# A four-layer graph attention kernel: sources listed from tile 1 on, 17 gather buffers, layer 0's masks kept beside its features

## The chip, the cores and the metric

One core of a Trainium2 chip runs the kernel. The metric is the device time of one execution in microseconds, as a median over runs; lower is better. Five engines work side by side, each in the order of its own instructions: PE multiplies matrices, DVE does elementwise work and reductions, ACT does activations and copies, POOL here mostly issues gathers, and SP issues the other transfers. Engines wait for one another through semaphores.

## The reference

A graph of 4,096 nodes with 256 features goes through four attention layers over one adjacency matrix. Edges are drawn with a probability that falls with both node numbers, so the first nodes have many neighbours and the late ones few. Each layer normalises the nodes, clips at zero, and adds the attention output to the nodes:

```python
_w = (1.0 + jnp.arange(4096)) ** -0.5
_w = _w / _w.mean()
adj = uniform((4096, 4096)) < clip(0.00390625 * _w[:, None] * _w[None, :], 0, 1)
...
h = jnp.maximum(_layernorm(x, axis=-1), 0.0)
...
h = node_features @ W.T + b_W
e = (h @ a1)[:, None] + (h @ a2)[None, :] + b_a[0]
e = jnp.where(e > 0, e, 0.2 * e)
scores = jnp.where(adjacency_matrix > 0, e, NEG_INF)
h_prime = jax.nn.softmax(scores, axis=1) @ h
...
x = x + h_prime
```

Layer 0 is the form shown. Layer 1 has no bias and puts an elu behind. Layer 2 has four heads of 64 features. Layer 3 takes a softmax of the scores and one of the negated scores, both over the projected inputs, and an elu; in the kernel these are two heads of 256.

## The kernel before

**Tiles.** 4,096 nodes are 32 tiles of 128 (NT), in 8 blocks of 512 targets (IB, NIB) and 8 chunks of four source tiles (CH, NCH). A node's row holds its features and, per head, two exponentials that stand in for the source's part of the score; `grow` holds the target's part, spread over partitions by a transpose on PE (L966) and an exponential on ACT (L972). One *step* takes 128 sources: DVE makes weights from `grow`, the row's exponential and a 0/1 mask (L1032; in layer 2 also ACT at L1018 and DVE at L1041 for two of the four heads), and PE multiplies them with the rows into an accumulator (L1068, in layer 2 L1093). A float32 matmul appears in the trace as two records.

**Dense blocks and listed tiles.** The first DENSE = (4, 2, 1, 1) target blocks of layers 0 to 3 are dense: they run over all 32 source tiles, 512 targets at a time. Every later target tile T is *listed*: it runs DP steps over the first DP source tiles, whose rows and masks lie in SBUF (`L.g` in layer 0, `L.pre` later, masks in `mpre`), and then CAPS[T] steps over lists of its actual sources. DP is 4, one chunk. `listed_sources` (L1208) fetches each list step with an indirect DMA on POOL (L1228): 128 rows of the layer's table in DRAM, at addresses from `index[T]`. A list shorter than its 128 x CAPS[T] places is filled with a row of zeros. If a list does not fit, a flag makes a slower program compute everything again.

**The lists.** While layer 0 runs, the adjacency arrives as int32 chunks (L1303), is made into bytes (L1322), stored to DRAM (L1324), and reduced to "does source p have any target in this tile" (L1329). From that `list_sources` (L819) counts places with matmuls, makes one-hot tiles on DVE (L875) in two halves of the JT = NT - DP source tiles, and multiplies them on PE (L900) into the index lists. These are used by all four layers.

**Masks.** A list step needs the 128 x 128 mask of its sources. For target blocks 1 to 3 the bytes lie beside the features in the tables of layers 1 and 2 (MASKS_IN, L473), so that one gather in the first listed layer of such a tile brings row and mask, and ACT copies the mask into `mlist` for later layers (L1240). For blocks 4 to 7, which are first listed in layer 0, masks lie in tensors of their own, `mask_t`; `gather_masks` (L922) fetches each with a second, small gather (L928), one per dense step ahead and the rest when the tile comes.

**Order.** `run` (L1191) walks a hand-written plan of (unit, step) pairs: fetch comes first, `begin` two, `weigh` three and `multiply` six plan places later (LEAD). POOL's instructions stand exactly in that order. In layer 0 the plan has 128 dense steps; from dense step LISTED0 = 40 on, each is followed by one or two listed steps in turn, and what is left runs alone. `sides` (L1284) says at which dense steps the chunks of blocks 4 to 7 are loaded: 2, 5, 8, ... 95. In layers 1 to 3 the plan starts with some dense steps alone (16, 36, 16) and spreads the rest over the first 24, 14 and 28 listed tiles; `all_sources` (L1413) streams their rows and masks chunk by chunk through SP, except for the first DP tiles. Gathered rows of layer 0 use a pool of 7 buffers (L1252), of layers 1 to 3 a pool of 9 (L1395). A buffer is free once PE, and where a mask is copied ACT, has read it.

Of the kernel before, what the change touches and what calls it, by code (L numbers as in the profile page):

```python
# [8 lines left out]
F32 = mybir.dt.float32  # L9
F16 = mybir.dt.float16  # L10
U8 = mybir.dt.uint8
# [6 lines left out]
P = 128  # L18
# [6 lines left out]
CH = 4  # L25
# [430 lines left out]
DP = CH  # L456
JT = NT - DP
TS0 = IT
# [3 lines left out]
LISTED0 = 40  # L462
CAPS = (25, 17, 15, 13, 12, 11, 11, 10, 10, 9, 9, 9, 8, 8, 8, 8) + (8,) + (7,) * 7 + (6,) * 8
# [9 lines left out]
MASKS_IN = {1: (2, False), 2: (1, False), 3: (1, True)}  # L473
FRONT = tuple(MW * ((l, False) in MASKS_IN.values()) for l in range(4))
TW = tuple(FRONT[l] + GW[l] + MW * ((l, True) in MASKS_IN.values()) for l in range(4))
# [4 lines left out]
def list_layers(ctx: ExitStack, tc: tile.TileContext, a: dict, out: bass.AP, flag):  # L480
# [29 lines left out]
    for T in range(TS0, NT):  # L510
# [8 lines left out]
    table = [dram.tile([N + 1, TW[l]], F32, name=f"table{l}", tag=f"table{l}") for l in range(4)]  # L519
    mask_t = {  # L520
        b: dram.tile([N + 1, IB], U8, name=f"mask_t{b}", tag=f"mask_t{b}")
        for b in range(NIB)
        if b not in MASKS_IN
    }
# [7 lines left out]
    def feature_rows(l, jt):  # L532
        return table_rows(table[l], jt)[:, :, FRONT[l] : FRONT[l] + GW[l]]

    def mask_rows(b, jt):
        if b not in MASKS_IN:
            return table_rows(mask_t[b], jt)
        l, behind = MASKS_IN[b]
        c0 = FRONT[l] + GW[l] if behind else 0
        return table_rows(table[l], jt)[:, :, c0 : c0 + MW].bitcast(U8)  # L540
# [6 lines left out]
    def weights(l, pool, prep, q):  # L547
# [11 lines left out]
        L.table = table[l]  # L559
# [123 lines left out]
    def node_rows(L, T0):  # L683
# [29 lines left out]
        for k, T in enumerate(tiles):  # L713
# [3 lines left out]
            hT = rows.tile([P, 2, P], F32, name=f"s_hT_{u}_{k}", tag="hT")  # L717
# [69 lines left out]
    def list_constants(pool):  # L787

        place = pool.tile([P, P, JT // 2], F16, name="place")
        nc.gpsimd.iota(  # L790
            place, pattern=[[1, P], [0, JT // 2]], base=0, channel_multiplier=0, allow_small_or_imprecise_dtypes=True
# [11 lines left out]
        n = (NT // 2 - DP) * IT  # L803
        for part, tiles, base in ((code[:, 0:n], NT // 2 - DP, DP * P - HALF), (code[:, n:], NT // 2, 1)):
            nc.gpsimd.iota(
                part,
                pattern=[[CH * P, tiles // CH], [1, CH], [0, IT]],
                base=base,
                channel_multiplier=CH,
                allow_small_or_imprecise_dtypes=True,  # L810
            )
# [7 lines left out]
    def list_sources(ib, seen, pool, consts):  # L819
# [3 lines left out]
        half = JT // 2  # L823
# [48 lines left out]
        def one_hot(T, j):  # L872

            first = pool.tile([P, P, half], F16, name=f"first_{T}_{j}", tag="first", bufs=2)
            nc.vector.tensor_tensor(  # L875
                first,
                place,
                lof[:, T % IT, j : j + half].unsqueeze(1).to_broadcast([P, P, half]),
# [5 lines left out]
        ahead = [(ib * IT + t, j) for t in range(IT) for j in (0, half)]  # L884
        firsts = [one_hot(*ahead[0])]
        yield 4.0
        for t in range(IT):
# [3 lines left out]
            for j in range(JT):  # L891
                if j % half == 0:
# [5 lines left out]
                if ps is None:  # L898
# [3 lines left out]
                    lhsT=first[:, :, j % half],  # L902
# [12 lines left out]

    masks_of = [
        (T, k)
        for T in range(DENSE[0] * IT, NT)
        for k in range(CAPS[T])
    ]  # L920

    def gather_masks(n, tile=None):  # L922

        for T, k in list(masks_of):
            if not n or tile is None and T not in index:
                break
            if tile in (None, T):
                nc.gpsimd.indirect_dma_start(  # L928
                    out=mlist[:, OFFS[T] + k, :],
                    out_offset=None,  # L930
                    in_=mask_t[T // IT],
                    in_offset=bass.IndirectOffsetOnAxis(ap=index[T][:, k : k + 1], axis=0),
                    element_offset=T % IT * P,
                )
                masks_of.remove((T, k))
                n -= 1

# [42 lines left out]
    class Unit:  # L980
# [4 lines left out]
        def __init__(u, L, T0, nt, n, get, big=None, heads=None, like=None, cost=1.7, nact=0, rates=(2, 0, 0), per=1):  # L985
# [205 lines left out]
    def run(plan):  # L1191

        n = len(plan)
        for p in range(n + LEAD[3]):
# [5 lines left out]
            if p >= LEAD[3]:  # L1200
# [4 lines left out]
                gather_masks(u.rates[2])  # L1205


    def listed_sources(L, T, pool):  # L1208
        heads = list(range(L.H))

        def get(i):
# [3 lines left out]
            else:  # L1215
# [4 lines left out]
                at, behind = MASKS_IN.get(T // IT, (0, False))  # L1220
                own = at == L.l > 0
                if at == 0:
                    gather_masks(CAPS[T], T)
# [7 lines left out]
                    in_=L.table,  # L1231
                    in_offset=bass.IndirectOffsetOnAxis(ap=index[T][:, k : k + 1], axis=0),
                    element_offset=FRONT[L.l] - front,
# [11 lines left out]
    with ExitStack() as phase:  # L1245
# [17 lines left out]
        def zero_rows():  # L1263
# [3 lines left out]
            for b in mask_t:  # L1267
                nc.sync.dma_start(mask_t[b][HALF : HALF + 1, :], zero[:, 0 : IB // 4].bitcast(U8))
            for l in range(4):
# [14 lines left out]
        sides = [2 + 3 * k for k in range((NIB - DENSE[0]) * NCH)]  # L1284
# [26 lines left out]
        def mask_chunk(ib, c):  # L1311

            load()
            if ib == 0:
                behind(c)
            m = (
                mpre[:, :, ib * IB : (ib + 1) * IB]
                if c == 0
                else mpool.tile([P, CH, IB], U8, name=f"s_m_{ib}_{c}", tag="m")
            )  # L1320
            for h, raw in enumerate(loaded[ib, c]):
                nc.vector.tensor_scalar(m[:, h * half : (h + 1) * half, :], raw, 0.0, None, op0=ALU.is_gt)  # L1322
            if c > 0 or ib in MASKS_IN:
                nc.sync.dma_start(mask_rows(ib, c * CH), m)  # L1324
            if ib > 0:
                if c == 0:
                    seen[ib] = lists_p.tile([P, JT, IT], F32, name=f"seen_{ib}", tag="seen", bufs=4)
                else:
                    nc.vector.tensor_reduce(  # L1329
                        seen[ib][:, (c - 1) * CH : c * CH, :].rearrange("p j t -> p (j t)"),  # L1330
                        m.rearrange("p j i -> p (j i)")
                        .bitcast(I32)
# [210 lines left out]
```

## Time and profile before

| | |
|---|---|
| median of 3 runs | 1810.38 us (1797.26 to 1814.76) |
| profiled execution | 1796.08 us, its span 1794.3 us |
| mean granted PE clock | 0.97 |
| PE, PE weight load, DVE, ACT, POOL busy | 93, 77, 74, 35, 54% |
| gathers of rows (L1228) | 715, mean 1060 ns on POOL |
| gathers of masks (L928) | 105, mean 1162 ns on POOL |
| copies of masks (L1240) | 113, mean 294 ns on ACT |
| steps on the fixed four tiles, DVE (L1032, 128x128) | 544 from `pre`, 64 from layer 0's `g` |
| DMA | 274.70 MB, mean 153 GB/s |

"Busy" is the share of the span in which an engine has an instruction under way. PE's matmuls are pipelined, so the duration of one record is longer than the time between two. POOL's time for a gather is the time in which it issues the transfer; the data land later.

### The profile page before, as it was taken

The numbers are of one execution on the slowest core, as the hardware profiler recorded it, in microseconds if no ns is written. First come the engines' busy times: TensorE is split into PE (matmuls) and PEld (weight loads), VectorE is DVE, ScalarE is ACT, GpSimd is POOL, SyncE is SP. The second block draws the span as 40 slices with busy tenths as digits, with TensorE's granted clock in tenths as the row PEclk, the third lists the DMA queues.
The fourth block names the chain that finished last, engine by engine and source line by source line (L and its number), as shares of the span: only waits on it lengthen the run. The fifth ranks groups of instructions, "written<-read, shape, count | busy, mean of one in ns | idle before, by whom it ended". The sixth has DMA issues, their size and how long they took to land.

```text
span 1794.3 us, 29158 instructions
## 1 busy us (share of the span) xinstructions
PE 1660.2 (93%) x9268; PEld 1384.3 (77%) x9268; DVE 1319.1 (74%) x3908; ACT 631.0 (35%) x1915; POOL 960.5 (54%) x930
## 2 busy tenths in 40 slices
PE   6998899799889999888999999988889999999997
PEld 4886777678778778676577878788888888888876
DVE  6787899777744676556788888877785566777755
ACT  5630010020120232333467666788884011111101
POOL 8836666646535656553353444444561666655453
PEclk9999999999879999989999999999999999999999
DMA  7888778853244444543233332323342665666553
GB/s 258 301 299 281 242 244 251 264 143 110 60 135 138 134 117 134 147 132 106 82 94 86 90 90 81 98 82 83 99 116 75 197 208 175 183 180 178 160 165 107
DMA packets 152237, 274.70 MB, mean 153 GB/s; under 512 B 21423, under 2 KB 75340, under 8 KB 152076
## 3 DMA queue, kind: packets, MB, share of 16 engines
q0 software_dynamic: 45584, 130.39, 26.8%
q1 hardware_dynamic: 105656, 141.83, 24.2%
q8 instruction: 77, 1.26, 0.3%
q14 instruction: 84, 0.69, 0.1%
q10 hardware_dynamic: 836, 0.53, 0.1%
HBM read 231.76 MB, written 40.90 MB: 152 GB/s over the span
## 4 chain that ended last, share of the span: by engine, by line
PE 78%; DVE 8%; issue 4%; DMA 3%; POOL 3%; ACT 2%; another core or an unknown queue 2%; SPq 0%; POOLq 0%; DVEq 0%; ACTq 0%
PE s_acc L1068 44%; PE s_accm L1093 20%; PE s_pj L748 8%; DVE s_p L1032 3%; PE idx_ps L900 2%; PE s_tp L716 2%; PE s_sT L966 2%; DMA s_gg<-table,idx 1%; DMA s_raw<-in_adjT 1%; ACT s_p L1018 1%; DVE s_m L1322 1%; POOL s_z L702 1%; POOL s_gg L1228 1%; DVE s_p L1041 0%
## 5 line engine op out<-in xcount | busy, mean ns | idle before, releaser
L1228 POOL DMA_INDIRECT s_gg<-table,idx x715 | 757.9, 1060 | 733.5 <-PE s_acc L1068 228.6
L1032 DVE SCALAR_TENSOR_TENSOR s_p<-s_grow,s_gg,mlist 128x128 f32<-128x128 f32 x994 | 310.1, 346 | 143.0 <-PE s_acc L1068 85.9
L1068 PE MATMUL s_acc<-s_gg,s_p 128*128 128x257 f32 x1430 | 353.8, 390 | 9.9 <-DVE s_p L1032 7.8
L1068 PEld LDWEIGHTS s_acc<-s_gg,s_p 128*128 128x128 f32 x1430 | 270.5, 194 | 53.6 <-DVE s_p L1032 12.6
L1068 PE MATMUL s_acc<-g,s_p 128*128 128x257 f32 x1152 | 292.5, 397 | 14.2 <-DVE s_p L1032 5.3
L1068 PEld LDWEIGHTS s_acc<-g,s_p 128*128 128x128 f32 x1152 | 220.0, 198 | 49.7 <-issue 12.3
L1032 DVE SCALAR_TENSOR_TENSOR s_p<-s_grow,pre,mpre 128x128 f32<-128x128 f32 (+1 forms) x576 | 189.2, 369 | 49.4 <-PE s_acc L1068 30.5
L1093 PE MATMUL s_accm<-s_p,s_gg 128*65 128x128 f32 x1744 | 204.7, 273 | 1.7 <-issue 1.6
L1068 PE MATMUL s_acc<-s_gs,s_p 128*128 128x257 f32 x896 | 203.6, 380 | 0.0
L1032 DVE SCALAR_TENSOR_TENSOR s_p<-s_grow,s_gs,s_ms 128x512 f32<-128x512 f32 x224 | 161.9, 748 | 50.7 <-PE s_accm L1093 24.7
L748 PE MATMUL s_pj<-s_w,s_hT 128*128 128x259 f32 (+3 forms) x640 | 175.9, 417 | 24.9 <-ACT s_hT L718 9.5
L1093 PEld LDWEIGHTS s_accm<-s_p,s_gg 128*65 128x65 f32 x1744 | 193.2, 138 | 5.3 <-issue 2.8
L1018 ACT ACTIVATE s_p<-s_grow,s_minus,s_gg 128x128 f32<-128x128 f32 x436 | 186.7, 485 | 25.9 <-PE s_accm L1093 15.0
L1068 PE MATMUL s_acc<-pre,s_p 128*128 128x257 f32 x768 | 184.0, 384 | 5.5 <-ACT s_y L1179 3.5
L1068 PEld LDWEIGHTS s_acc<-s_gs,s_p 128*128 128x128 f32 x896 | 169.4, 190 | 24.7 <-issue 0.6
L972 ACT ACTIVATE s_grow<-s_sT 128x256 f32<-128x256 f32 (+2 forms) x136 | 46.8, 367 | 379.3 <-PE s_sT L966 260.9
L748 PEld LDWEIGHTS s_pj<-s_w,s_hT 128*128 128x128 f32 x640 | 126.3, 205 | 56.4 <-ACT s_hT L718 14.2
L1068 PEld LDWEIGHTS s_acc<-pre,s_p 128*128 128x128 f32 x768 | 144.5, 192 | 28.4 <-ACT s_y L1179 3.9
L928 POOL DMA_INDIRECT mlist<-mask_t,idx x105 | 122.1, 1162 | 65.1 <-issue 30.0
L1093 PE MATMUL s_accm<-s_p,pre 128*65 128x128 f32 (+1 forms) x928 | 122.2, 286 | 2.6 <-issue 2.5
L1093 PEld LDWEIGHTS s_accm<-s_p,pre 128*65 128x65 f32 x928 | 105.1, 139 | 21.0 <-issue 18.3
L1018 ACT ACTIVATE s_p<-s_grow,s_minus,pre 128x128 f32<-128x128 f32 x224 | 95.0, 485 | 23.2 <-issue 18.9
(126 smaller groups left out, 1743.5 us busy)
## 6 DMA issues: line engine op xcount, KB each, us to landing
s_raw<-in_adjT SPq DMA_DIRECT2D x128, 512.0 KB
s_gs<-table SPq DMA_DIRECT2D x28, 516.0 KB
s_gg<-table,idx POOLq DMA_INDIRECT x715
mask_t<-s_m SPq DMA_DIRECT2D x35, 256.0 KB
table<-s_g SPq DMA_DIRECT2D x28, 258.0 KB
s_ms<-mask_t SPq DMA_DIRECT2D x28, 256.0 KB
table<-s_m SPq DMA_DIRECT2D x21, 256.0 KB
table<-g SPq DMA_DIRECT2D x8, 516.0 KB
```

The lines of the kernel that those rows point to most:

```text
L702: (nc.gpsimd if L.l == 0 else nc.vector).tensor_scalar(z, x[:, T, :], mv[:, k, 0:1], 0.0, op0=ALU.subtract, op1=ALU.max)
L716: nc.tensor.transpose(tp[:, c, :], zs[k][:, c * P : (c + 1) * P], ident)
L748: nc.tensor.matmul(ps, lhsT=hT[:, c, :], rhs=L.w[:, c, k * (D + 6) : k * (D + 6) + cols], start=(c == 0), stop=(c == 1),)
L900: nc.tensor.matmul(ps[:, 0:cap], lhsT=first[:, :, j % half], rhs=val[:, 0:cap, j * IT + t], start=(j == 0), stop=(j == JT - 1),)
L928: nc.gpsimd.indirect_dma_start(out=mlist[:, OFFS[T] + k, :], out_offset=None, in_=mask_t[T // IT], in_offset=bass.IndirectOffsetOnAxis(ap= ...
L966: nc.tensor.transpose(ps[:, h - h0, it, :], L.s[:, T0 + it, h : h + 1].to_broadcast([P, P]), ident)
L972: nc.scalar.activation(grow[:, h1:h2, :], ps[:, h1 - h0 : h2 - h0].rearrange("p h a b -> p h (a b)"), AF.Exp, scale=scale,)
L1018: nc.scalar.activation(w[:, h, :], u.grow[:, h, :], AF.Relu, scale=g[h][:, n - 1 : n], bias=minus)
L1032: nc.vector.scalar_tensor_tensor(p[:, k, :], u.grow[:, h, :], g[k][:, n - 1 : n], m, op0=ALU.min if L.l == 3 and h == 1 else ALU.max, op1= ...
L1068: nc.tensor.matmul(u.accs[it][h], lhsT=p[:, k, it * P : (it + 1) * P], rhs=g[k][:, 0:n], start=first, stop=last,)
L1093: nc.tensor.matmul(u.regions[h], lhsT=g[k][:, 0 : DH + 1], rhs=p[:, k, :],  start=first and (u.nt > 1 or h == 0), stop=last, skip_group_ch ...
L1228: nc.gpsimd.indirect_dma_start(out=wide, out_offset=None, in_=L.table, in_offset=bass.IndirectOffsetOnAxis(ap=index[T][:, k : k + 1], axis=0),
```

## The change

DP goes from 4 to 1: only source tile 0 is fixed, and lists start at tile 1. CAPS grows by up to three places a tile, JT from 28 to 31. Layer 0's features are stored in two DRAM tables instead of one, table 0 and a fifth, table 4; beside them lie the masks of blocks 4 and 5, and 6 and 7. Layer 0's gathers fetch mask and row together, and ACT copies the mask to `mlist`; `gather_masks` goes. Layer 0's listed steps start at dense step 48 and come by two after odd steps and in the last quarter. The dense blocks of layers 1 to 3 stream all chunks. Gather buffers of layers 1 to 3 go from 9 to 17, those of `hT` from 2 to 4. Line numbers behind the cut move up by some 25 to 30.

```diff
-DP = CH
+DP = 1
 JT = NT - DP
+HALFT = (JT + 1) // 2
-LISTED0 = 40
-CAPS = (25, 17, 15, 13, 12, 11, 11, 10, 10, 9, 9, 9, 8, 8, 8, 8) + (8,) + (7,) * 7 + (6,) * 8
+LISTED0 = 48
+CAPS = (28, 20, 17, 16, 14, 13, 13, 12, 12, 11, 11) + (10,) * 4 + (9,) * 5 + (8,) * 8 + (7,) * 4
...
-MASKS_IN = {1: (2, False), 2: (1, False), 3: (1, True)}
+MASKS_IN = {1: (2, False), 2: (1, False), 3: (1, True), 4: (0, False), 5: (0, True), 6: (4, False), 7: (4, True)}
+LAYER = (0, 1, 2, 3, 0)
...
-            hT = rows.tile([P, 2, P], F32, name=f"s_hT_{u}_{k}", tag="hT")
+            hT = rows.tile([P, 2, P], F32, name=f"s_hT_{u}_{k}", tag="hT", bufs=4)
...
+            n = min(HALFT, JT - j)
+            first = pool.tile([P, P, HALFT], F16, name=f"first_{T}_{j}", tag="first", bufs=2)
             nc.vector.tensor_tensor(
-                first,
-                place,
-                lof[:, T % IT, j : j + half].unsqueeze(1).to_broadcast([P, P, half]),
+                first[:, :, 0:n],
+                place[:, :, 0:n],
+                lof[:, T % IT, j : j + n].unsqueeze(1).to_broadcast([P, P, n]),
...
-                at, behind = MASKS_IN.get(T // IT, (0, False))
-                own = at == L.l > 0
-                if at == 0:
-                    gather_masks(CAPS[T], T)
+                at, behind = MASKS_IN[T // IT]
+                own = LAYER[at] == L.l
+                at = at if own else L.l
...
-                    in_=L.table,
+                    in_=table[at],
...
-        sides = [2 + 3 * k for k in range((NIB - DENSE[0]) * NCH)]
+        sides = [2 + 3 * k - k // 8 for k in range((NIB - DENSE[0]) * NCH)]
...
-            m = (
-                mpre[:, :, ib * IB : (ib + 1) * IB]
-                if c == 0
-                else mpool.tile([P, CH, IB], U8, name=f"s_m_{ib}_{c}", tag="m")
-            )
+            m = mpool.tile([P, CH, IB], U8, name=f"s_m_{ib}_{c}", tag="m")
...
-            if c > 0 or ib in MASKS_IN:
-                nc.sync.dma_start(mask_rows(ib, c * CH), m)
+            nc.sync.dma_start(mask_rows(ib, c * CH), m)
+            if ib == 6:
+                ensure(lambda: all(L0.ready[c * CH : (c + 1) * CH]))
+                nc.sync.dma_start(feature_rows(4, c * CH), L0.g[:, c * CH : (c + 1) * CH, :])
             if ib > 0:
...
+                    nc.scalar.copy(mpre[:, :, ib * IB : (ib + 1) * IB], m[:, 0:DP, :])
...
-                if ib * NT + step[1] >= LISTED0:
-                    n = 1 + step[1] % 2
+                at = ib * NT + step[1]
+                if at >= LISTED0:
+                    n = 2 if at % 2 or at >= dense_steps * 3 // 4 else 1
...
-    gat = ctx.enter_context(tc.tile_pool(name="s_gather", bufs=9))
+    gat = ctx.enter_context(tc.tile_pool(name="s_gather", bufs=17))
...
-                if jt < DP:
-                    ensure(lambda: L.ready[jt])
-                    return mine, [L.pre[:, jt, h * n : (h + 1) * n] for h in mine], mpre[:, jt, w]
```

## The prediction

> **What bounds the kernel now.** I read the page's busy times, then the chain that ended last, then the busy times cut at the four layers (my cuts: 522, 841 and 1365 us, where PE's matmuls change from one layer's to the next), and last the groups with shapes kept apart.
>
> ```profile
> PE 1660.2 (93%) x9268; PEld 1384.3 (77%) x9268; DVE 1319.1 (74%) x3908; ACT 631.0 (35%) x1915; POOL 960.5 (54%) x930
> ...
> PE 78%; DVE 8%; issue 4%; DMA 3%; POOL 3%; ACT 2%; another core or an unknown queue 2%; SPq 0%; POOLq 0%; DVEq 0%; ACTq 0%
> ```
>
> PE carries the chain; POOL and DMA have 3% each. By layer (columns: window, length, then PE, PEld, DVE, ACT and POOL busy with counts, granted clock, DMA share, GB/s):
>
> ```profile
> 0.00:522.00 522.00, 462.86 (x2588) 384.20 (x2588) 405.98 (x1047) 118.06 (x427) 324.63 (x320) 0.94 0.69 215
> 522.00:841.00 319.00, 287.64 (x1292) 240.35 (x1292) 191.88 (x583) 82.95 (x297) 173.95 (x174) 0.95 0.48 137
> 841.00:1365.00 524.00, 497.35 (x3474) 403.37 (x3473) 440.80 (x1390) 376.73 (x1053) 233.30 (x218) 0.99 0.32 89
> 1365.00:1794.30 429.30, 412.35 (x1920) 356.37 (x1918) 280.45 (x891) 53.22 (x139) 228.59 (x218) 0.99 0.56 167
> ```
>
> PE is over 90% busy after layer 0; in layer 2 DVE (84%) stands beside it. POOL is at 55, 45 and 53% in layers 1 to 3. The groups that the change touches:
>
> ```profile
> L1228 POOL DMA_INDIRECT s_gg<-table,idx x715 | 757.9, 1060 | 733.5 <-PE s_acc L1068 228.6 <-PE s_accm L1093 128.4 <-issue 103.2
> L1068 PE MATMUL s_acc<-pre,s_p 128*128 128x257 f32 x768 | 184.0, 384 | 5.5 <-ACT s_y L1179 3.5 <-issue 1.1 <-DVE s_rz L1182 0.9
> L1032 DVE SCALAR_TENSOR_TENSOR s_p<-s_grow,pre,mpre 128x128 f32<-128x128 f32 x544 | 166.6, 347 | 47.8 <-PE s_acc L1068 30.3 <-PE s_accm L1093 8.7 <-issue 4.0
> L928 POOL DMA_INDIRECT mlist<-mask_t,idx x105 | 122.1, 1162 | 65.1 <-issue 30.0 <-DVE s_rz L1121 26.1 <-DVE idx L910 4.6
> L1240 ACT COPY mlist<-s_gg 128x128 uint8<-128x128 uint8 x113 | 32.7, 294 | 70.1 <-DMA s_gg<-table,idx 65.1 <-issue 4.4
> L875 DVE TENSOR_TENSOR first<-place,lof 128x1792 f16<-128x1792 f16 x56 | 60.8, 1085 | 7.1 <-PE idx_ps L900 4.1 <-PE s_acc L1068 2.9
> ```
>
> The `pre` rows are steps that every listed tile runs on the fixed sources, four each, sparse or not. POOL mostly waits for PE to free a gather buffer. Its own pace shows where nothing holds it:
>
> ```profile
> 1391.15 0.94 POOL L1228 DMA_INDIRECT s_gg<-table,idx  x1 [0.30 <-PE s_acc L1068]
> 1392.40 0.95 POOL L1228 DMA_INDIRECT s_gg<-table,idx  x1 [0.30 <-issue]
> ```
>
> So 1.25 us apiece at best; with the mean of 1.06 plus 0.30 it is 1.36 (layer 1: 173.95/174 + 0.30 = 1.30; layer 3: 228.59/218 + 0.30 = 1.35). The end of layer 0 is a place of its own:
>
> ```profile
> 480.00:495.00 15.00, 13.05 (x79) 10.71 (x80) 10.31 (x31) 2.48 (x9) 6.18 (x6) 0.51 0.21 49
> 495.00:510.00 15.00, 15.00 (x77) 12.34 (x77) 5.87 (x26) 4.81 (x18) 10.11 (x10) 0.70 0.27 67
> ```
>
> Here the dense steps have run out, listed steps stand alone, and the clock is 0.51 and 0.70.
>
> **What the Trainium skill says.** "Perfetto Trace Analysis", Identifying the Most-Contended Engine: matmul busy time is no measure of the distance from peak. The trace agrees: a 128x257 record lasts 384 ns, yet from 1395 to 1710 us 1,470 records fill 314.0 us, 0.214 each. A float32 matmul is two records (1,430 for the 105 + 174 + 2 x 218 = 715 on gathered rows), so I price one at 0.424 us, not 0.77. "TensorE: Matmul & The Clock Gate", Part 1: an idle array falls to half clock and needs sustained work to leave it; the 0.51 above agrees. "DMA: Bandwidth & Descriptors", Anatomy of one DMA — SWDGE: about 2 us of every such DMA is fixed completion time; the trace has gathers on its chain in pieces of 3 to 5 us, so depth of buffers, not speed, hides it. "VectorE: DVE Perf Modes", tier table: a 16-bit `tensor_tensor` does two elements a cycle; 1,792 in 1.085 us agrees.
>
> **Part by part.**
>
> *Fewer listed steps (DP 4 to 1, larger CAPS).* A tile runs DP + CAPS steps. Summing the tuples: layer 0 169 to 144, layer 1 270 to 235, layers 2 and 3 330 to 291. Gathers go 105 to 128, 174 to 211, 218 to 263 and 218 to 263.
> - Layer 0: 25 x 0.424 = -10.6 us of PE, 25 x 0.31 = -7.8 of DVE.
> - Layer 1: 35 x 0.424 = -14.8 on PE. But POOL needs 211 x 1.30 = 274 us from about 537 (its first gather), ending near 811 to 830; PE without the steps would end at 826. Both are close: I take -12 (bounds -18 and +5).
> - Layer 2: PE 8 records of 0.109 (24 in 2.62 us in the chain) = 0.87 us a step; DVE 2 x 0.31 + 0.42 = 1.04; ACT 2 x 0.43 = 0.86. DVE sets it: 39 x 1.04 = -41. In the last 14 tiles no dense steps are left: 128 gathers x 1.37 = 175 us against 142 steps at 1.04 to 1.2, 148 to 170, so POOL gives some back: -36 (bounds -45, -20).
> - Layer 3: two matmuls a step, 39 x 0.85 = -33. POOL 263 x 1.35 = 355 us from about 1390, ending near 1745, against PE's 1790 - 33 = 1757: just inside. -28 (bounds -38, -10).
>
> *17 buffers.* No work; it lets POOL run 17 gathers (some 23 us) ahead, which is what makes the above hold. Alone it removes waits on buffers (228.6 + 128.4) that PE does not feel.
>
> *Layer 0's masks in the tables.* Removes 105 mask gathers (122.1 us of POOL), so POOL's gathers in layer 0 fall from 210 to 128; no PE time there, since the wait on POOL is not on the chain. Adds 128 ACT copies x 0.29 = 37 us; ACT is at 118 of 522, hidden unless they block a `grow` behind them (layer 1 has 65.1 us of such ACT waits, at most some 15 us of PE idling near them). SP: 8 more feature stores of 516 KB, 5 more mask stores, 28 mask stores that become 512-byte pieces, and 10 chunk loads in the later layers. Their DMA time: 4.2 MB at the 300 GB/s of the early slices is 14 us, the five masks 4, pieces and wider gathers perhaps 20, less the 105 gathers. From 45 to 360 us the DMA share is 0.77 to 0.89, and `s_raw` is on the chain: +8 (0 to +25). Gathers wait for all earlier stores to their table; starting at step 48 instead of 40 puts that behind them.
>
> *Longer lists.* 84 more index matmuls (784 cost 55.7 us): +6 PE. One-hots of 2,048 and 1,920 elements: 28 x 0.133 + 28 x 0.067 = +5.6 DVE, `val` +2.9, seven more reductions +3.7. If the rows of 15 lose the two-element rate, +28 more. DVE is 78% busy in layer 0, so its net +4 is mostly covered.
>
> *Order of layer 0.* Listed steps left alone after the dense ones: 169 - 132 = 37 before, 144 - 136 = 8 after. From 480 to 522, 182 records (84 of them index matmuls) are 27 us of PE work in 42 us; -10 (bounds -20, 0).
>
> *Chunk 0 streamed.* Five more loads each of `gs` and `ms`. At layer 1's start the first load was issued at 521.2 and first used at 527.1 behind chunk 0, which lay in SBUF; uncovered now: +3 (0 to +6). Layers 2 and 3 have it stored long before: 0. `hT` with four buffers: 0 to -3.
>
> **Sum**: layer 0 -10.6 + 6 + 8 - 10 + 3 = -3 to -4; -12; -36; -28: about -79 on the profiled 1796.1, so 1717. The median shown, 1810.4, is 0.8% above that execution: 1731.
>
> **Rivals.**
> 1. *Likeliest, 0.62*: as summed, 1700 to 1760 as a median.
> 2. *Layer 0 gives it back, 0.22*: ACT copies queued before `grow`, slower one-hots and more DMA cost 30 to 45 us there. For it: DMA 0.85 early. Against: DVE waits only 9.7 us for `s_raw`. 1731 + 38 = about 1770.
> 3. *POOL becomes the bound and it is slower, 0.07*: layers 1 and 3 then last 15 + 211c and 35 + 263c against 319 and 429 us. With -30 left from layer 2 the change is 474c - 728 us: nothing at c = 1.54 us a gather, slower above. Layer 0 shows single gathers of 1.5 to 2.3 us while DMA is loaded. Against: layer 3 has 1.35 at a DMA share of 0.62. At 1.65 us: +54, 1864.
> 4. *The steps removed were hidden, 0.09*: if PE's slack absorbs them, within 1%, about 1805. Against: PE's records are back to back in layer 3.
>
> **Numbers.** 1731 us; 1690 to 1785 takes in case 1 whole and most of 2. Under 1% cannot be told from no change: the three runs spread by 1%. Faster 0.84, within 1% 0.09, slower 0.07.
>
> **What would show it.** Layer spans near 518, 307, 488 and 401; POOL busy near 70% in layers 1 and 3 (211 x 1.0 of 307, 263 x 1.05 of 401); `pre` groups a quarter of their counts; no `mlist` gathers; no clock of 0.5 at layer 0's end. Wrong if POOL's mean gather exceeds 1.2 us, if `DVE s_p` waits on gathers by more than some 60 us, or if layer 0 grows.

## The result and the profile after

The changed kernel takes 1900.09 us (median of 4 runs, 1897.51 to 1909.96) against 1803.82 for the kernel before beside it: ratio 1.054, 95% interval 1.046 to 1.062, so **slower**. Forecast were 1731 us and a range of 1690 to 1785. The profiled execution took 1899.61 us with a span of 1897.7, 103.4 more than before's.

A kernel's time here depends on the occasion: the kernel before took 1804 us beside the changed one and 1790 beside the first four experiments, but 1699 to 1700 beside the other eleven, so times are compared only with those measured beside them.

The page after, its busy times and its chain:

```profile
PE 1636.5 (86%) x8764; PEld 1341.1 (71%) x8764; DVE 1265.1 (67%) x3660; ACT 643.3 (34%) x1994; POOL 999.2 (53%) x976
...
PE 60%; issue 6%; DVE 4%; DMA 3%; ACT 3%; another core or an unknown queue 2%; POOL 1%; POOLq 0%; DVEq 0%; ACTq 0%
```

PE is busy for 24 us less, and carries 60% of the chain in place of 78%. It now stands idle for 261 us of 1897.7, before for 134 of 1794.3. By layer (window, length, busy PE, PEld, DVE, ACT and POOL with counts, clock, DMA share, GB/s):

```profile
0.00:561.00 561.00, 478.40 (x2639) 395.52 (x2639) 420.10 (x1035) 158.71 (x575) 227.70 (x239) 0.91 0.76 227
561.00:905.50 344.50, 283.29 (x1206) 231.47 (x1207) 179.32 (x543) 81.95 (x297) 211.48 (x211) 0.91 0.49 140
905.50:1432.60 527.10, 478.50 (x3166) 382.62 (x3165) 411.36 (x1275) 349.33 (x983) 278.91 (x263) 0.95 0.37 103
1432.60:1897.70 465.10, 396.30 (x1757) 331.47 (x1755) 254.34 (x809) 53.34 (x139) 281.15 (x263) 0.94 0.62 182
```

From here on layer 0 ends at layer 1's first attention matmul, which in the profile of before is at 526.2, 4 us behind the prediction's cut. So layers took 526, 315, 524 and 429 us before and 561, 345, 527 and 465 after: **+35, +29, +3 and +37**. The groups that the change touched:

```profile
L1205 POOL DMA_INDIRECT s_gg<-table,idx x865 | 921.2, 1065 | 859.8 <-PE s_acc L1047 212.5 <-issue 147.2 <-PE s_accm L1072 124.7
L1217 ACT COPY mlist<-s_gg 128x128 uint8<-128x128 uint8 x263 | 76.6, 296 | 332.3 <-DMA s_gg<-table,idx 319.9 <-issue 11.4
L1047 PE MATMUL s_acc<-pre,s_p 128*128 128x257 f32 x160 | 51.6, 428 | 36.5 <-issue 18.8 <-ACT s_y L1158 13.4 <-DVE s_y L1163 2.5
L877 DVE TENSOR_TENSOR first<-place,lof 128x2048 f16<-128x2048 f16 x28 | 36.0, 1285 | 18.1 <-PE idx_ps L902 18.1
L877 DVE TENSOR_TENSOR first<-place,lof 128x1920 f16<-128x1920 f16 x28 | 35.0, 1249 | 0.0
```

The edits did what they say: 865 gathers at 1.065 us (before 1.060), 211 + 263 + 263 of them in layers 1 to 3, a quarter or less of the `pre` steps, no gathers into `mlist`. Two things stand out. ACT waits 320 us for gathers ahead of its mask copies (before 65). And the first matmuls of listed tiles wait for "issue", which says that the profile shows nothing they wait for.

**What such a wait is.** Layer 3's timeline around the second longest one (start, duration, engine, instruction, idle time before it and what ended it):

```profile
1468.38 2.19 PE L1047 MATMUL s_acc<-s_gg,s_p 128*128 128x257 f32 x8
...
1476.53 0.94 POOL L1205 DMA_INDIRECT s_gg<-table,idx  x1 [0.30 <-issue]
1479.33 0.52 SPq L1404 DMA_DIRECT2D s_gs<-table  x1
1479.34 0.61 DVE L1011 SCALAR_TENSOR_TENSOR s_p<-s_grow,s_gg,mlist 128x128 f32<-128x128 f32 x2 [12.41 <-remote]
1479.74 1.36 PEld L1047 LDWEIGHTS s_acc<-s_gg,s_p 128*128 128x128 f32 x4 [9.86 <-issue]
1479.74 3.79 PE L1047 MATMUL s_acc<-s_gg,s_p 128*128 128x257 f32 x8 [9.17 <-issue]
...
1481.24 0.38 ACT L951 ACTIVATE s_grow<-s_sT 128x256 f32<-128x256 f32 x1 [27.88 <-PE s_acc L1047]
1481.27 0.94 POOL L1205 DMA_INDIRECT s_gg<-table,idx  x1 [3.79 <-PE s_acc L1047]
```

PE's last matmul ends at 1470.57. SP, DVE, ACT and POOL, which all wait on PE's counter, start at 1479.33 to 1481.27. The trace's semaphore records give the reason: for the counter, which otherwise rises 0.01 us after the matmul, no rise is recorded between 1465.22 and 1479.31, the latter 8.7 us after PE's last matmul had ended, and eleven more rises come 0.042 us apart from 1480.88 to 1481.30. The matmuls that raise it end 0.43 us apart here. So, although a matmul's end is modelled in these records, the signals had been held up and not the work. The row that DVE stood before had landed at about 1466.4 (the sixteen completion packets of each gather tell this). I call these **late signals**. Adding up the longest delay of each episode of over 1 us, without the program's end, gives 29, 23, 13 and 4 us in layers 0 to 3 before, and 3, 29, 24 and 42 after. How large such sums are depends on when an episode counts as over: with 3 us free of lateness they are 35, 24, 15 and 4, and 3, 33, 27 and 55, in the same order. (The sums of layer 3 in the expectations below hold another 13 us or so from the program's very end, which nearly every run has.)

### The profile page after: what moved, and what is told of

Same layout as the page of the kernel before. It is cut to its first block, busy times and chain, and to the rows that moved or that the text cites. A ratio compares the mean times of both kernels' runs of the same rounds, so it can differ in the third digit from the quotient of the medians.

```text
span 1897.7 us, 28326 instructions
## 1 busy us (share of the span) xinstructions
PE 1636.5 (86%) x8764; PEld 1341.1 (71%) x8764; DVE 1265.1 (67%) x3660; ACT 643.3 (34%) x1994; POOL 999.2 (53%) x976
## 4 chain that ended last, share of the span: by engine, by line
PE 60%; issue 6%; DVE 4%; DMA 3%; ACT 3%; another core or an unknown queue 2%; POOL 1%; POOLq 0%; DVEq 0%; ACTq 0%
PE s_acc L1047 32%; PE s_accm L1072 19%; PE s_pj L746 6%; DMA s_gg<-table,idx 3%; PE s_sT L945 1%; DVE s_p L1011 1%; ACT s_p L997 1%; PE s_tp L714 1%; PE idx_ps L902 1%; POOL s_gg L1205 1%; PE s_oT L1134 1%; ACT s_grow L951 0%; ACT mlist L1217 0%; ACT s_g L781 0%
## 5 line engine op out<-in xcount | busy, mean ns | idle before, releaser
L1205 POOL DMA_INDIRECT s_gg<-table,idx x865 | 921.2, 1065 | 859.8 <-PE s_acc L1047 212.5
L1047 PE MATMUL s_acc<-s_gg,s_p 128*128 128x257 f32 x1730 | 446.8, 402 | 38.9 <-DVE s_p L1011 21.3
L1047 PEld LDWEIGHTS s_acc<-s_gg,s_p 128*128 128x128 f32 x1730 | 336.1, 201 | 102.2 <-DVE s_p L1011 29.1
L1072 PE MATMUL s_accm<-s_p,s_gg 128*65 128x128 f32 x2104 | 261.9, 280 | 12.8 <-issue 12.8
L1217 ACT COPY mlist<-s_gg 128x128 uint8<-128x128 uint8 x263 | 76.6, 296 | 332.3 <-DMA s_gg<-table,idx 319.9
L1011 DVE SCALAR_TENSOR_TENSOR s_p<-s_grow,s_gg 128x128 f32<-128x128 f32 x315 | 101.0, 343 | 52.6 <-PE s_acc L1047 15.6
L1072 PE MATMUL s_accm<-s_p,s_gs 128*65 128x512 f32 x256 | 115.9, 592 | 0.0
L1293 DVE TENSOR_SCALAR s_m<-s_raw 128x1024 uint8<-128x1024 int32 x128 | 91.0, 722 | 31.0 <-DMA s_raw<-in_adjT 30.3
L1011 DVE SCALAR_TENSOR_TENSOR s_p<-s_grow,g,s_m 128x512 f32<-128x512 f32 x128 | 96.4, 763 | 3.2 <-PE s_acc L1047 2.6
L1020 DVE SCALAR_TENSOR_TENSOR s_p<-s_p,mlist 128x256 f32<-128x256 f32 x211 | 87.4, 414 | 11.5 <-ACT s_p L997 9.7
```

The costliest lines, as they stand in the source:

```text
L1011: nc.vector.scalar_tensor_tensor(p[:, k, :], u.grow[:, h, :], g[k][:, n - 1 : n], m, op0=ALU.min if L.l == 3 and h == 1 else ALU.max, op1= ...
L1020: nc.vector.scalar_tensor_tensor(p[:, own:, :], p[:, own:, :], 1.0, m.unsqueeze(1).to_broadcast([P, u.nact, w]), op0=ALU.add, op1=ALU.mult,)
L1047: nc.tensor.matmul(u.accs[it][h], lhsT=p[:, k, it * P : (it + 1) * P], rhs=g[k][:, 0:n], start=first, stop=last,)
L1072: nc.tensor.matmul(u.regions[h], lhsT=g[k][:, 0 : DH + 1], rhs=p[:, k, :],  start=first and (u.nt > 1 or h == 0), stop=last, skip_group_ch ...
L1205: nc.gpsimd.indirect_dma_start(out=wide, out_offset=None, in_=table[at], in_offset=bass.IndirectOffsetOnAxis(ap=index[T][:, k : k + 1], ax ...
L1217: nc.scalar.copy(kept, m)
```

## The experiments

Layers in us, cut alike; a dash separates kernels run beside different measurements of before.

| run | median | ratio to before, 95% | layers 0, 1, 2, 3 |
|---|---|---|---|
| before, first profile | 1803.82 | | 526, 315, 524, 429 |
| after, first profile | 1900.09 | 1.046 to 1.062 | 561, 345, 527, 465 |
| - beside before at 1789.98 | | | |
| e1, 9 buffers | 1865.39 | 1.035 to 1.047 | 557, 357, 513, 441 |
| e2, POOL pauses | 1880.38 | 1.045 to 1.056 | 562, 346, 520, 452 |
| e3, copy later | 1885.41 | 1.047 to 1.061 | 555, 340, 526, 456 |
| e4, masks gathered, 9 buffers | 1883.63 | 1.047 to 1.058 | 583, 352, 513, 437 |
| - beside before at 1699.70 | | | |
| e5, spare gathers | 1716.50 | 1.007 to 1.014 | 487, 297, 493, 434 |
| e6, spare memsets | 1704.25 | 1.001 to 1.004 | 490, 297, 492, 424 |
| e7, no masks, 9 buffers | 1721.95 | 1.009 to 1.018 | 504, 309, 492, 414 |
| e8, 13 buffers | 1728.58 | 1.012 to 1.022 | 557, 309, 464, 395 |
| - beside before at 1699.00 | | | |
| e9, after again | 1725.19 | 1.013 to 1.017 | 559, 308, 465, 394 |
| e10, stores only, 13 | 1685.53 | 0.990 to 0.994 | 520, 309, 463, 396 |
| e11, copies on DVE, 13 | 1696.11 | 0.997 to 1.000 | 527, 308, 467, 395 |
| e12, masks gathered, 13 | 1714.45 | 1.006 to 1.013 | 542, 308, 466, 394 |
| - beside before at 1698.58 | | | |
| e13, spare gathers in two layers | 1729.37 | 1.015 to 1.019 | 490, 298, 509, 435 |
| e14, 6 buffers | 1895.46 | 1.114 to 1.123 | 555, 361, 531, 448 |
| e15, copies on DVE, 17 | 1691.70 | 0.995 to 0.997 | 524, 307, 464, 395 |

**Depth and pauses where signals are late.** e1 changes one number:

```diff
-    gat = ctx.enter_context(tc.tile_pool(name="s_gather", bufs=17))
+    gat = ctx.enter_context(tc.tile_pool(name="s_gather", bufs=9))
```

> The changed kernel with 9 buffers for gathered rows in layers 1 to 3 in place of 17. Theory A: POOL issuing gathers without ever having to wait holds up PE's semaphore signals, so that DVE, SP and ACT start up to 9 us late; 9 buffers make POOL stop every 9 gathers. Then the five waits of layer 3 (9.2, 9.6, 6.4, 6.3, 4.0 us) go, layer 3 falls from 465 to 405-430 us, layer 1 from 344 to 315-330, and the whole from 1900 to 1820-1850. Theory B: the rate or the latency of the gathers is the bound, since the steps on fixed sources no longer cover it; then fewer buffers leave PE waiting more: 1900 or above.

Layer 3 fell by 24 us and layer 2 by 14, less than theory A asked, and layer 1 rose by 12. The late signals went from 24 to 14 us in layer 2 and from 42 to 16 in layer 3, but from 29 to 45 in layer 1. Part of this is the occasion: e3 below has the change's own instructions in layer 3, and beside the same before that layer took 456 us with 29 us of late signals, so 15 of the 24 us are left to e1. With 17 buffers a row of layer 3 had lain landed for 11.3 us on average when DVE took it; with 9 for 1.35, and 147 of 263 for under 1 us. So rows bind at 9 buffers, as theory B says, and not at 17, where the rows are there and the signals are not.

e2 leaves the 17 buffers and makes POOL do something else:

```diff
+                if L.l and k % 4 == 3:
+                    nc.gpsimd.memset(pause, 0.0)
```

> The changed kernel, 17 buffers, with a memset of 128x256 floats (some 0.5 us) on POOL after every fourth gather of a list in layers 1 to 3. It costs POOL about 170 x 0.6 = 100 us and frees no buffer. Theory A: signals drain while POOL does something other than issue gathers, so the stalls of layer 3 shrink: 1830-1870. Theory B: POOL's pace is the bound, so it gets slower: layer 3 by some 263/4 x 0.6 = 40 us, the whole to 1950-2000. If signals drain only while POOL waits, no change or a little slower: 1890-1950, with the same pattern of late signals.

Layer 3 fell by 13 us against the first profile, but by 4 against e3's; the interval overlaps that of the change itself. Theory B's loss of 40 us is refuted. Theory A's gain did not come either: the late signals of layers 1 to 3 are 36, 17 and 29 us, where e3 has 39, 21 and 29.

What speaks for POOL's gathers is where in POOL's work the late signals fall. Of PE's signals recorded within 1.3 us after a gather's start, the share that came over 0.1 us late, by how many gathers POOL had issued with no wait between (gaps under 0.45 us):

| gathers in a row | 1 to 2 | 3 to 5 | 6 to 9 | 10 and more |
|---|---|---|---|---|
| before | 0.04 | 0.23 | 0.65 | 0.58 (24 signals) |
| after | 0.16 | 0.24 | 0.47 | 0.70 (64) |
| e1, 9 buffers | 0.11 | 0.18 | 0.44 | 0.62 (24) |
| e2, POOL pauses | 0.25 | 0.37 | 0.50 (36) | none |
| after again, e9 | 0.00 | 0.00 | 0.00 | 0.00 (1045) |

Where signals are late, the share rises with the length of the run. But e2's pauses cut the runs of layers 1 to 3, and what they took from the long runs came back as a higher share in the short ones, so the count of gathers in a row is not shown to be the cause. In e9, the same kernel on another occasion, no signal is late in runs of up to 207 gathers.

**Layer 0.** e3 moves ACT's mask copy behind three plan places:

```diff
-                    nc.scalar.copy(kept, m)
+                    copies[L.l, T, i] = kept, m
...
+            if (L.l, u.T0, i) in copies:
+                nc.scalar.copy(*copies.pop((L.l, u.T0, i)))
```

> The changed kernel with 17 buffers, where ACT's copy of a gathered mask is issued at the step's weighing instead of at its fetch, three plan places later, so that ACT no longer stands waiting for the gather's landing (256.8 us of such waits in layer 0, 61.1 in layer 1). Theory C: these waits hold target rows and features queued behind them on ACT and so cost layer 0 much of its +39 us: layer 0 falls from 561 to 525-545, the whole to 1865-1885. If layer 0 is lost to something else (the late first gather, the transfers): 1895-1905.

Layer 0 at 555 was 6 us better, too little to tell, and the ratio did not move. ACT still stood 249.5 us in front of gathers in that layer, so the edit had not taken the wait away, and this run says nothing on what the wait costs.

e4 brings layer 0's masks as before, each with a gather of its own:

```diff
-MASKS_IN = {1: (2, False), 2: (1, False), 3: (1, True), 4: (0, False), 5: (0, True), 6: (4, False), 7: (4, True)}
+MASKS_IN = {1: (2, False), 2: (1, False), 3: (1, True)}
...
+                if at == 0:
+                    gather_masks(CAPS[T], T)
```

> One fixed source tile and 9 buffers as in the run of the changed kernel with 9 buffers, but layer 0's masks in tensors of their own and gathered by themselves (128 of 1.16 us on POOL, no copies on ACT, no second feature table), as before the change. Theory C (the masks beside the features lose layer 0's time): layer 0 at 515-530 against 561, and 30-45 us below the 9-buffer run. Theory D (layer 0 is lost to the longer lists, the start at step 48 and the order of listed steps): layer 0 within 10 us of the 9-buffer run's.

Both theories missed: layer 0 took 583, 26 more than in e1. Its late signals rose from 3 to 41 us, with 256 gathers in the layer in place of 128.

e7 leaves the masks of layer 0's lists out and keeps the rest of e4:

```diff
-                nc.gpsimd.indirect_dma_start(
-                    out=mlist[:, OFFS[T] + k, :],
...
+                nc.vector.memset(mlist[:, OFFS[T] + k, :], 1)
```

> One fixed source tile, 9 buffers, layer 0's masks neither in the tables nor gathered: the 128 x 128 masks of blocks 4 to 7's lists are left out and set to one by DVE (some 10 us in sum), so every listed source counts for every target of its tile. It shows what layer 0 costs without any way of bringing masks. Theory E (bringing the masks, in either way, is what layer 0 lost): layer 0 at 505-530 against 557 with tables and 583 with mask gathers. Theory D (longer lists and the order of listed steps): 550 or above.

Layer 0 took 504 us (e6, whose layers 0 to 2 are those of the kernel before: 490; changed: 559). Theory E holds: without any way of bringing masks the layer is within 14 us of before, and 55 of the 69 us go with bringing them. The 14 us are a balance: e7 has the longer lists, the new order and 19.0 us of DVE for setting masks, but it also lacks the 105 mask gathers of before, whose cost in time no run here isolates.

e10 adds the stores back, but no fetch:

```diff
-                more = 0 if not own else (T % IT + 1 if behind else IT - T % IT) * MW // IT
+                more = 0 if not own or L.l == 0 else (T % IT + 1 if behind else IT - T % IT) * MW // IT
...
+                if own and L.l == 0:
+                    nc.vector.memset(m, 1)
```

> The changed kernel with 13 buffers; layer 0's masks and features are stored in the two tables as there, but layer 0's gathers fetch rows alone, no mask is copied, and the 128x128 masks of those lists are left out (set to one by DVE, as in the run without masks). What is left against that run are the stores: masks in 512-byte pieces and the second feature table. Theory F (the stores' transfers hold up the loads of adjacency, DMA share 1.0 from 80 to 240 us): layer 0 at 535-560 on a chip where without masks it took 504 and with all 557. Theory G (the fetch of masks with the rows and the copies are the loss): 505-520.

520: the stores (masks in pieces and the second feature table) cost 16 us, and the fetch with its copies the 37 up to the 557 of e8, below. e11 then moves the copies to DVE:

```diff
-                    nc.scalar.copy(kept, m)
+                    copies[L.l, T, i] = kept, m
...
             u.steps[i] = heads, g, p
+            if (L.l, u.T0, i) in copies:
+                nc.vector.tensor_copy(*copies.pop((L.l, u.T0, i)))
```

> The changed kernel with 13 buffers, and the 211 copies of gathered masks (layers 0 to 2) moved from ACT at the fetch to DVE behind the step's own weighing, where the rows have landed already: some 0.1-0.15 us each, 20-30 us of DVE. ACT no longer stands behind a gather (237 us in layer 0, 77 in layer 1). Theory C: layer 1 falls from 309 to 290-300 and layer 0 from 557 to 535-550, 20-35 us in all against 13 buffers (ratio to before near 1.00). If ACT's waits are only time in which it had nothing else to do: ratio 1.015-1.02 as with 13 buffers.

Layer 0 fell from 557 to 527, more than expected, though a copy took DVE 0.235 us (e15, with 263 copies in all) and not 0.1 to 0.15; layer 1 did not move. So the copies on ACT were 30 of the 37 us. Two windows of layer 0 show the two losses apart. First e9, the change itself, from 80 to 240 and from 240 to 400 us:

```profile
80.00:240.00 160.00, 137.24 (x768) 114.32 (x768) 130.44 (x275) 33.40 (x114) 41.12 (x36) 0.92 0.99 301
240.00:400.00 160.00, 135.65 (x777) 112.53 (x777) 124.78 (x310) 35.34 (x131) 58.31 (x49) 0.90 0.76 234
```

e15, the same with copies on DVE:

```profile
80.00:240.00 160.00, 139.41 (x769) 114.82 (x768) 133.90 (x298) 26.55 (x90) 43.83 (x35) 0.91 0.98 299
240.00:400.00 160.00, 151.23 (x938) 128.44 (x937) 145.45 (x406) 29.11 (x104) 68.87 (x57) 0.96 0.83 254
```

e10, with the stores but without fetch and copies, in the first window, and e7, without the stores, in both:

```profile
80.00:240.00 160.00, 139.93 (x778) 117.02 (x777) 136.51 (x315) 28.01 (x96) 44.77 (x37) 0.91 0.98 299
...
80.00:240.00 160.00, 146.79 (x883) 123.64 (x882) 150.19 (x348) 31.72 (x108) 55.36 (x43) 0.98 0.91 297
240.00:400.00 160.00, 144.16 (x864) 121.73 (x863) 135.43 (x338) 25.01 (x90) 67.80 (x59) 0.95 0.74 228
```

In the first window the DMA share is 0.98 to 0.99 with the stores and 0.91 without, at the same 300 GB/s, and PE has 768 to 778 records in place of 883; e10 shows that the stores alone do this. Transfers bind there. Whether it is the masks' 512-byte pieces or the second feature table, whose stores take the place of loads, was not separated. In the second window, moving the copies gives 938 records for 777. One of the places, on ACT in e9:

```profile
358.59 0.30 ACT L1217 COPY mlist<-s_gg 128x128 uint8<-128x128 uint8 x1 [1.17 <-DMA s_gg<-table,idx]
364.29 0.30 ACT L1217 COPY mlist<-s_gg 128x128 uint8<-128x128 uint8 x1 [5.41 <-DMA s_gg<-table,idx]
364.50 0.26 ACT L768 ACTIVATE s_g<-s_pj,s_r 128x2 f32<-128x2 f32 x1
```

and on PE:

```profile
360.71 0.59 PE L1047 MATMUL s_acc<-s_gg,s_p 128*128 128x257 f32 x2
365.65 0.32 PE L945 MATMUL s_sT<-s_ident,s_s 128*128 128x128 f32 x1 [4.34 <-ACT s_g L781]
```

ACT stands 5.4 us before a copy for a row that is still to come. The features behind it in ACT's order (L768 to L781) are ready by then, and PE waits 4.3 us for them. In all, ACT stands 256 us before copies in layer 0 of e9; in e15 DVE stands 14 us before the same copies.

e12 combines mask gathers, 13 buffers and copies on DVE (in layers 1 and 2):

> A version put together from what gained: one fixed source tile, 13 buffers, layer 0's masks in tensors of their own and gathered by themselves, the copies of blocks 1 to 3's masks (layers 1 and 2) on DVE behind the weighing. On a chip without late signals: layer 0 at 505-525, layer 1 at 290-300, layers 2 and 3 at 464 and 395 as with 13 buffers, so 1660-1685, 1-2% below before. On a chip with late signals the 128 mask gathers and the longer runs hold up PE, as in the earlier run with 9 buffers (1884 against 1790): 1.04-1.06 of before.

A miss: layer 0 took 542, 38 more than without masks, though no signal was late. The 256 gathers of the layer are 287 us of POOL, with waits between; why they cost more than the 210 of before is open.

**Gathers as such.** e5 and its control e6 add work on POOL to layer 3 of the kernel before:

```diff
+                if L.l == 3 and k % 3 == 2:
+                    nc.gpsimd.indirect_dma_start(
+                        out=spare[k // 3 % 4],
...
+                        in_offset=bass.IndirectOffsetOnAxis(ap=index[T][:, k : k + 1], axis=0),
```

> The kernel before with 65 spare gathers in layer 3: ahead of every third gather of a list POOL gathers 128 single values that nobody reads. POOL had 229 us of work in 429 us there; 65 x 1.25 = 81 us more still leave it idle for over 100 us, and next to no bytes are moved. Theory A (back-to-back gathers hold up PE's signals): layer 3 grows by 10-35 us and its late signals grow from 16 us in sum to over 30. Theory B (only the supply of rows counts): layer 3 stays within 5 us of before, or grows only where rows come less than 1 us before their use.

e6, in the same place:

```diff
+                    for _ in range(2):
+                        nc.gpsimd.memset(spare, 0.0)
```

> The control for the spare gathers: at the same 65 places POOL writes zeros into a spare tile twice (2 x some 0.55 us), so it is as busy but issues no more gathers. If it is the gather that holds up PE's signals: no change from before (within 0.5%). If any work that keeps POOL from waiting does it, or POOL's time itself: as much slower as with the spare gathers.

No signal was late in either. With memsets the whole kept within 0.5%, as expected of a cost that lies in gathers. With spare gathers layer 3 took 434 us, with memsets 424. The 10 us are of the size that theory A gave as its least, but came without late signals, so they count against it. e13 puts them into layer 2 as well:

> The kernel before with spare gathers of 128 single values ahead of every third gather of a list in layers 2 and 3 (130 in all, some 163 us of POOL, hardly any bytes). Where PE's signals come in time (before near 1700): layer 3 grows by about 10 us as with the spare gathers there alone, layer 2, where POOL has 233 us of work in 524, by 0-10: ratio 1.01-1.02. Where signals come late (before near 1790-1800): theory A expects more late signals in layers 2 and 3 than the 13 and 16 us in sum of the first profile of before, and a ratio of 1.02-1.05.

Layer 3 grew to 435 as in e5, layer 2 from 492 to 509, more than expected; the ratio is in the range given. A gather costs something where POOL has 100 us to spare: one of 128 single values took 1.035 us on POOL in e5, as long as one of rows (1.048), and rows behind it come later: in layer 3 DVE waits 57.7 us for gathers in e5, 40.0 in e6, and in layer 2 of e13 ACT waits 15.7 us for them before its mask copies.

**Depth where signals are on time.** e8 has 13 buffers:

> The changed kernel with 13 buffers. With 9, layer 3 is held by the supply (147 of 263 rows are used within 1 us of landing) and takes 441 us; with 17, by late signals, and takes 465. Theory A: in between, both are smaller: layer 3 at 430-450, the whole at 1850-1880 on the scale where 9 buffers gave 1865. Without such a trade the time falls or rises evenly from 9 to 17.

and e9 is the change with its 17:

> The changed kernel as it is, once more, beside the next three runs. On the chip of the last four runs the kernel before took 1700 us and no signal of PE was late outside layer 3's end; on the earlier chip it took 1790 to 1804, with late signals in every layer. If late signals belong to the chip, then where the kernel before is near 1700 the changed one is within 5-40 us of it (13 buffers: 1729), with layer 0 near 557, layers 1 to 3 near 309, 464, 395; where before is near 1800, the changed one is near 1900 with layers as in its first profile.

and e14 has 6:

> The changed kernel with 6 buffers. Where signals come in time, depth is all that counts: layer 3 at 425-450 against 414 with 9 and 395 with 13, layer 2 at 500-515, the whole 30-70 us above the 17-buffer one (1.03-1.05 of before). Where they come late, theory A expects runs of at most 6 gathers to leave few late signals in layers 2 and 3 (under 10 us in sum each, against 24 and 55 with 17 buffers), while rows arrive just in time: 1.03-1.06.

Layer 3 takes 448, 414 (e7), 395 and 394 us with 6, 9, 13 and 17 buffers, layer 2 531, 492, 464 and 465. Six cost far more than expected: DVE waited 331 us for gathers in layers 1 to 3. There is no optimum between 9 and 17 here; theory A's trade needs late signals. e9 settles that these belong to the occasion: beside a before of 1699 the change costs 1.5%, not 5.4%. The chip's number does not tell occasions apart: e1 to e4, with late signals, and e5 to e8, without, are both on record as chip 6. The layers of e9:

```profile
0.00:559.20 559.20, 477.95 (x2639) 395.80 (x2639) 418.12 (x1035) 158.63 (x575) 231.82 (x239) 0.91 0.75 227
559.20:867.30 308.10, 263.72 (x1206) 223.70 (x1207) 181.04 (x543) 82.38 (x297) 209.60 (x211) 0.93 0.55 157
867.30:1332.50 465.20, 457.18 (x3166) 367.48 (x3165) 405.06 (x1275) 347.38 (x983) 287.35 (x263) 1.00 0.42 117
1332.50:1726.80 394.30, 376.62 (x1757) 324.57 (x1755) 262.12 (x809) 53.24 (x139) 261.33 (x263) 0.99 0.71 215
```

and those of e6, which stands for the kernel before (in layer 3 with its memsets):

```profile
0.00:489.70 489.70, 450.80 (x2600) 376.89 (x2601) 408.79 (x1054) 119.65 (x431) 322.59 (x320) 0.98 0.75 233
489.70:787.10 297.40, 277.02 (x1281) 235.81 (x1281) 189.03 (x577) 81.31 (x292) 174.27 (x174) 0.97 0.50 142
787.10:1279.20 492.10, 487.30 (x3478) 400.70 (x3477) 437.48 (x1391) 379.40 (x1053) 237.26 (x218) 1.00 0.35 95
1279.20:1703.60 424.40, 410.50 (x1913) 353.84 (x1911) 282.63 (x889) 53.22 (x139) 263.69 (x348) 0.99 0.58 169
```

With signals on time the change is worth **+69, +11, -27 and -30 us** by layer. In layers 2 and 3 PE is idle for 8 and 18 us; in the first profile after it was idle for 49 and 69 there, and busy 21 and 20 us longer, at clocks of 0.95 and 0.94 for 1.00 and 0.99.

**The copies off ACT, at 17 buffers.** e15 is the change with its copies on DVE:

> The changed kernel, 17 buffers as in the change, with the copies of gathered masks on DVE behind the weighing instead of on ACT at the fetch. Where signals come in time: as with 13 buffers (0.998 of before), 0.993-1.000, since rows wait longer in their buffers. Where they come late: 30 us below the changed kernel's 1.054, so 1.035-1.045.

1691.7 us, 0.4% below the kernel before (0.995 to 0.997), a tenth of what was forecast for the change, and 1.9% below the change measured beside a before of the same time. It was not measured where signals are late.

## Why the prediction was wrong

The size of the result, +103 us in the profiled runs, is +23 that the change costs with signals on time (e9 against e6: 1726.8 less 1703.6; 26 by the medians of e9 and of before beside it, as e6 has its memsets), and +80 more: on the first occasion the changed kernel's profile was 171 us longer (1897.7 against 1726.8), and that of before only 91 (1794.3 against 1703.6, e6 again standing for it). By layer these are 36, 18, 32 and 4 us before and 2, 36, 62 and 71 after, large and small roughly where the sums of late signals (29, 23, 13, 4 and 3, 29, 24, 42) are. The sums come to 69 of the 91 us and 98 of the 171, so late signals go with the loss and do not account for all of it.

**Layer 0, the first step that failed** (forecast -4, measured +35, with signals on time +69). The term was "ACT copies +37 us, hidden unless they block a `grow` behind them", priced at nothing. They block: 30 to 35 us (e8 to e11, e9 to e15). The count of 128 x 0.29 us was right and the wrong quantity: ACT stands 256.8 us before its copies, over 112 waits, and what stands behind is not only a `grow` but also the next layer's features. The stores, priced at +8 (0 to +25), cost 16. The lists, with the tail, were -10.6 + 6 - 10, about -15: e7 has +14, but with 19.0 us of DVE for setting masks and without the mask gathers of before, so how far this term itself was off is not shown. The tail's clock of 0.51 that was to go is still there (535 to 550 us: 0.51). The one-hots kept their rate: 1.285 us for 2,048 elements, 1.249 for 1,920, together 71.0 us against 60.8, so +10 where +5.6 were forecast. (Every second tile took 1.35 and 1.28 us, the others 1.22; in the former, by the source, a row of `lof` starts at an odd element. Before, with rows of 28, all took 1.08.) Rival 2 had the mechanism by name. Its 38 us above the forecast's -4 happen to be the +35 of the first profiles, where before lost 36 us of layer 0 to the occasion and the change 2; they are half of what the change costs without that.

**Layer 1** (forecast -12, bounds -18 to +5; measured +29, with signals on time +11). "Both are close: I take -12" chose the wrong one of two bounds. In e9 the 211 gathers run from 561.0 to 847.6, 1.36 us apiece, with 14 us of waits beyond the 0.30 before each, so POOL sets the end:

```profile
690.78 0.95 POOL L1205 DMA_INDIRECT s_gg<-table,idx  x1 [0.30 <-issue]
692.03 0.95 POOL L1205 DMA_INDIRECT s_gg<-table,idx  x1 [0.30 <-PE s_acc L1047]
693.28 1.07 POOL L1205 DMA_INDIRECT s_gg<-table,idx  x1 [0.30 <-DVE s_p L1011]
```

Idle 0.30 before each is its own pace, whatever the releaser's name. 211 x 1.36 and some 20 us from the last gather to the layer's end are the 308. All seven kernels with this list and 9 or more buffers took 307 to 309 where signals were on time, wherever the copies were. So rival 3's mechanism held, in this one layer and below its break-even of 1.54 us. The other 18 of the first profiles' +29 are what the occasion added to the changed kernel (36) beyond before (18).

**Layers 2 and 3** (forecast -36 and -28; measured +3 and +37). With signals on time they are -27 and -30, both inside the bounds given, and the layers last 465 and 394 where 488 and 401 were forecast on a slower before. So the sums of steps were right. What the sum has no term for is the late occasion, which adds 62 and 71 us to these layers and 32 and 4 to those of before. In the prediction's terms the step is "*17 buffers.* No work", priced at nothing: the late occasion adds 61 and 62 us with 17 buffers (e3 against e9) and 21 and 27 with 9 (e1 against e7); in layer 1 it is the other way round, 32 and 48. So the depth goes with the loss in layers 2 and 3; that POOL's longer runs hold up the signals, or that fewer steps on fixed sources leave PE less to do meanwhile, is argued and not shown. Of the forecast's own signs, a mean gather of over 1.2 us did not come: it stayed at 1.065. DVE waits on gathers were 26.4 us in the first profile, under the 60 named, but 75.4 in e9. Layer 0 did grow.

**What was in the profile of before and not read.** Its waits in layer 0 hold "ACT s_hT <- remote: 27.0, 4, 9.7" (engine and tile, us in total, times, longest). ACT waits for a transpose on PE of under a microsecond, and yet 9.7 us at a time, released by nothing that is named. These waits end as late signals arrive, 29 us of which lie in that layer.

**Open.** What makes an occasion one with late signals was not found. That POOL's gathers hold them up rests on the table by runs and on e1; no run with late signals tested it by spare gathers, as signals were on time whenever these were tried, e1 has layer 1 against it, and e2's pauses changed nothing.

## What to carry to other kernels

A copy that waits for a transfer is not priced by its own 0.3 us but by what is queued behind it while its engine stands: 256 us of standing cost 30 to 35 us in layer 0, and some 77 us (e8) cost nothing in layer 1, where POOL set the end. Putting it on an engine that needs the data anyway took that price away here. Steps that look like wasted work may be the time in which another engine issues its transfers: before taking them out, set each stage's count of issues times their measured pace beside the stage's time, and where the two are within a few per cent, forecast the worse. Waits released by "remote" or "issue" that are far longer than the work they wait for deserve a look at the semaphore records before any sum is made.

## What the runs showed of the hardware

- PE's signals came 8.7 us and more after the matmul's end while its own work was done (first profile after, 1470.57 to 1479.31); the backlog then drained 0.042 us apart. The same kernel on another occasion had none, and was 9% faster (1900 to 1725).
- A gather's cost on POOL did not depend on its bytes: 1.035 us for 128 single values, 1.048 for 128 rows (e5), and 0.30 between two.
- With masks stored in 512-byte pieces and a second feature table the DMA share was 0.98 at 299 GB/s (e10, 80 to 240 us), where without them 297 GB/s took 0.91 (e7).
